# Finishing a block of nodes in stages, and scaling a relation's product after the matmul: a four-layer graph network on one core

## The chip, the core and the metric

The kernel runs on one core of a Trainium2 chip. Its engines are TensorE (PE in the profile, with its weight loads as PEld), VectorE (DVE), ScalarE (ACT), GpSimd (POOL) and SyncE (SP); each works through its own instructions in order. The metric is the device time of one execution in microseconds. Before the change its median over three runs is 2428.57 us (2426.19 to 2432.78).

## What is computed

Four graph layers over 3125 nodes of 128 features and 53,125 edges sorted by destination, each with a residual and a layer norm. Layer 0 is a GIN block of four rounds; layers 1 to 3 sum, for each destination node, what its edges bring by relation. Cut to the core:

```
x = layernorm(x + gin(x))                                  # 4 x: h = x + segment_sum(x[src], dst); relu(h W1 + b1) W2 + b2
# layer 1: mean per relation
out = x @ root + bias
for r in range(8):
    s = segment_sum((x @ W[r])[src] * (type == r), dst)
    c = segment_sum(type == r, dst)
    out = out + s / maximum(c, 1)
x = layernorm(x + relu(out))
# layer 2: relation weights from 8 bases, an attention factor per relation; x @ update once per edge of dst
x = layernorm(x + relu(layer2(x)))
# layer 3: messages (x[src] @ W[r] + bias_term[r]) * gate, plus x @ loop_weight
x = layernorm(x + relu(layer3(x)))
```

In layers 1 to 3 the kernel first sums the source rows per destination and relation (or basis) and multiplies by the relation's matrix afterwards, once per node instead of once per edge.

## The kernel before

A first part (`gnn_kernel`) tests that the edges are in order; they are, so `in_order` runs, and the other path (`any_order`) does not. `gin_layers` does layer 0: it builds the adjacency in SBUF as BF16 (lines 668 to 698) and multiplies densely (`dense`, line 598). It ends by writing the table `fx0` (`xtab[0]`) to HBM.

**One relational layer** (`relational`, line 945) walks over 416 tiles of 128 edges. For each tile GpSimd gathers the 128 source rows from the layer's table (line 915); four tiles share one buffer `xg`, and there are six such buffers, so gathers can run 24 tiles ahead. VectorE makes a one-hot `oh` of 128 edges by 16 destinations x 8 relations (lines 1003, 1005, 1010 for layers 1, 2, 3), TensorE multiplies (`pw`, line 1012, three PSUM buffers), and VectorE adds the 128x128 product into `sums` at a column offset read from a register (line 1014). `sums` holds features x (node, relation) for all nodes. Layers 1 and 3 also count edges (or sum gates) per node and relation on TensorE, `pc` at line 1020, from one-hots made by `hots` (line 918) for eight tiles at a time; the records show two per product, as for every FP32 matmul here.

**One block** is 128 nodes; there are 25 (24 full ones and one of 53). A block is complete after the last tile that can hold one of its destinations (`last_tile`, line 766). At that tile the loop at line 1022 calls the layer's `finish`, which emits everything for the block at once:

- `finish1` (line 1046): load the block's own rows `xb` (SP), copy the counts (ScalarE), reciprocals of max(count, 1) for 8 relations x 128 nodes; spread these over all partitions with eight selector matmuls (`sel`, line 1057) in two PSUM halves, and scale `sums` into `sc` (line 1058); turn the rows (`turned`, line 936); then one accumulation in PSUM: root, bias, and eight products (`by_relation`, line 1031); `normed` (line 1039) with residual and layer norm; store to `fx1`.
- `finish2` (line 1113): the same pattern without counts of its own; it multiplies by the update matrix and eight bases, norms, turns the result again, makes the gates of layer 3 (line 1126 on) and stores 136 columns to `gtab`.
- `finish3` (line 1135): loop weight, bias by summed gates, eight products, norm, store to the output.

After a block the loop clears the part of `sums` of the block before it (line 1026, `clear` on ScalarE). Layer 2's gathers read the table that layer 1's blocks write, all rows of it, so a layer's first gather waits for the last block's store.

The code is written in one order, and the framework then sets each engine's order of instructions, when the program is built, from dependencies and its own estimates of time. So instructions of a block's finish can stand between those of tiles, and the counts of layer 1 stand well ahead of the tiles that they belong to.

Of the kernel before, what the change touches and what calls it, by code (L numbers as in the profile page):

```python
# [58 lines left out]
NSEG = NB  # L59
NR = 8  # L60
DGRP = 16
DRIFT = 40.0
PADDST = 4095

# [701 lines left out]
def last_tile(c1):  # L766

    return max(t for t in range(TE) if low(t)[0] < c1)
# [8 lines left out]
def in_order(ctx: ExitStack, tc: tile.TileContext, a: dict, out: bass.AP, pre: dict):  # L777
# [31 lines left out]
    def clear(b, engine=nc.scalar.copy):  # L809
        engine(sums[:, b * P * NR:(b + 1) * P * NR], zero.to_broadcast([P, P * NR]))  # L810
# [29 lines left out]
    def load(name, shape, src):  # L840
        t = const.tile(shape, src.dtype, name="f_" + name)
        nc.sync.dma_start(t, src)
        return t
# [3 lines left out]

    rW = load("rW", [P, R8, D], a["L1_gnn_W"].rearrange("r i o -> i r o"))
    root = load("root", [P, D], a["L1_gnn_root"])
    rbias = load("rbias", [1, D], a["L1_gnn_bias"].rearrange("(a o) -> a o", a=1))  # L850
    sel = const.tile([R8, R8, P], F32, name="f_sel")
    cnt = const.tile([R8, NP], F32, name="f_cnt")
    zeroh = const.tile([1, SEGN + 2 * W], BF16, name="f_zeroh")
    nc.vector.memset(zeroh, 0.0)
# [60 lines left out]
        nc.gpsimd.indirect_dma_start(out=dst, out_offset=None, in_=table,  # L915
                                     in_offset=bass.IndirectOffsetOnAxis(ap=idx, axis=0))

    def hots(keys_, n, name, t):

        m = min(GRP, TE - t)  # L920
        oh = wk.tile([P, GRP, n], F32, name=name)
        nc.vector.tensor_tensor(oh[:, :m], iota[:, :n].unsqueeze(1).to_broadcast([P, m, n]),
                                keys_[:, t:t + m].unsqueeze(2).to_broadcast([P, m, n]), OP.is_equal)
        return oh
# [20 lines left out]
    def relational(layer, table, width, finish, beside=lambda t: None):  # L945
        counted = layer in (1, 3)
        segs, cgroups = {}, {}
        b = 0

        def coefficients(t):  # L950

# [13 lines left out]
        for t in range(TE):  # L965
# [4 lines left out]
            if t % GRP == 0:  # L970
                m = min(GRP, TE - t)
                if counted:
                    r8 = hots(et8, R8, "h8", t)
                    hw = hots(dlr, W, "hw", t)
                    spot = []
                    for i in range(2):
                        us = [u for u in range(t, t + m) if len(segments(u)) > i]
                        us = range(us[0], us[-1] + 1) if us else us
                        spot.append(dict(zip(us, values(seg[0:1, i, us[0]:us[-1] + 1], PE, [spots(u, i) for u in us]))) if us else {})
                else:  # L980
                    if t == 0:
                        coefficients(0)
                    if t + GRP < TE:
                        coefficients(t + GRP)
# [15 lines left out]
            for u, x, r, gate in ready:  # L1000
                oh = ohp.tile([P, W * NR], F32, name="oh")
                if layer == 1:
                    nc.vector.tensor_scalar(oh, iota[:, :W * NR], key8[:, u:u + 1], None, op0=OP.is_equal)  # L1003
                elif layer == 2:
                    nc.vector.scalar_tensor_tensor(  # L1005
                        oh.rearrange("p (d b) -> p d b", b=NR), W2["dcol"], dlr[:, u:u + 1],
                        cgroups[u - u % GRP][:, u % GRP, :].unsqueeze(1).to_broadcast([P, W, NBASE]),
                        op0=OP.is_equal, op1=OP.mult)
                else:
                    nc.vector.tensor_scalar(oh, iota[:, :W * NR], key8[:, u:u + 1], gate, op0=OP.is_equal, op1=OP.mult)  # L1010
                ps = psum.tile([P, W * NR], F32, name="pw", bufs=3)
                nc.tensor.matmul(ps, x[:, u % 4, :D], oh, start=True, stop=True)  # L1012
                w = sums[:, bass.ds(place[u % DGRP], W * NR)]
                nc.vector.tensor_tensor(w, ps, w, OP.add)  # L1014
                if counted:
                    for i, j in enumerate(segments(u)):
                        if j not in segs:
                            segs[j] = psum.tile([R8, SEGN + 2 * W], F32, name="pc", bufs=2)
                            nc.tensor.matmul(segs[j], zeroh[:, :R8], zeroh, start=True, stop=False)
                        nc.tensor.matmul(segs[j][:, bass.ds(spot[i][u], W)], r, hw[:, u % GRP, :], start=False,  # L1020
                                         stop=u == last_tile(min(N, (j + 1) * P)))
                while b < NB and u == last_tile(min(N, (b + 1) * P)):
                    finish(b, sums[:, b * P * NR:(b + 1) * P * NR].rearrange("p (d r) -> p r d", r=NR),
                           segs[b][:, W:W + P] if counted else None)
                    if layer < 3 and b > 0:
                        clear(b - 1)
                    b += 1
        if layer < 3:
            clear(NB - 1)

    def by_relation(s, w, first):

        pb = psum.tile([P, D], F32, name="pm", bufs=2)
        first(pb)
        for r in range(NR):
            nc.tensor.matmul(pb, s[:, r, :], w[:, r, :], start=False, stop=r == NR - 1)  # L1036
        return pb

    def normed(pb, xb, dst):

        r = wk.tile([P, 1, D], F32, name="res")
        nc.vector.scalar_tensor_tensor(r[:, 0, :], pb, 0.0, xb, op0=OP.max, op1=OP.add)
        layer_norm(nc, wk, eps, r, dst, P, 1)


    def finish1(b, s, pc):
        blk = slice(b * P, (b + 1) * P)
        xb = rows_of(xtab[0], b)
        nc.scalar.copy(cnt[:, blk], pc)
        ci = wk.tile([R8, P], F32, name="ci")  # L1050
        nc.vector.tensor_scalar(ci, cnt[:, blk], 1.0, None, op0=OP.max)
        nc.vector.reciprocal(ci, ci)
        sc = wk.tile([P, R8, P], F32, name="sc", bufs=1)
        for h in range(0, R8, BPB):
            pr = psum.tile([P, BANK], F32, name="pr", bufs=1)
            for r in range(BPB):
                nc.tensor.matmul(pr[:, r * P:(r + 1) * P], sel[:, h + r, :], ci, start=True, stop=True)  # L1057
            nc.vector.tensor_tensor(sc[:, h:h + BPB, :], s[:, h:h + BPB, :], pr.rearrange("p (r d) -> p r d", d=P), OP.mult)  # L1058
        xt = turned(xb)

        def first(pb):
            nc.tensor.matmul(pb, xt, root, start=True, stop=False)
            nc.tensor.matmul(pb, ones[0:1, :], rbias, start=False, stop=False)

        y = wk.tile([P, 1, D], F32, name="y")
        normed(by_relation(sc, rW, first), xb, y)
        nc.sync.dma_start(xtab[1][blk, :], y[:, 0, :])

    def beside1(t):
        if t == 0:  # L1070
            clear(1)
        if t == 4:
            nc.vector.tensor_copy(sel, ident[:R8, :R8].unsqueeze(2).to_broadcast([R8, R8, P]))
        if t == 120:
            later_weights()
        for b in range(2, NB):
            if t == max(1, first_tile(b * P) - GRP):
                clear(b)
# [34 lines left out]
    def finish2(b, s, _):  # L1113
        blk = slice(b * P, (b + 1) * P)
        xb = rows_of(xtab[1], b)
        xt = turned(xb)
        pd = psum.tile([P, P], F32, name="pm", bufs=2)
        nc.tensor.matmul(pd, ones[:R8, :], cnt[:, blk], start=True, stop=True)
        xd = wk.tile([P, P], F32, name="xd")
        nc.vector.tensor_tensor(xd, xt, pd, OP.mult)  # L1120
        pb = by_relation(s, W2["bases"], lambda pb: nc.tensor.matmul(pb, xd, W2["upd"], start=True, stop=False))
        yg = wk.tile([P, 1, GX], F32, name="yg")
        normed(pb, xb, yg[:, :, :D])
        xt = turned(yg[:, 0, :D])
        pg = psum.tile([P, P], F32, name="pm", bufs=2)
        nc.tensor.matmul(pg[:, :R8], xt, W2["V"], start=True, stop=True)
        gs = wk.tile([P, R8], F32, name="gs")
        nc.vector.tensor_tensor(gs, pg[:, :R8], W2["gconst"], OP.add)
        nc.scalar.activation(yg[:, 0, D:], gs, AF.Sigmoid)
        nc.sync.dma_start(gtab[blk, :], yg[:, 0, :])  # L1130

    relational(2, xtab[1][:, :], D, finish2)

# [1 line left out]
    def finish3(b, s, pc):  # L1135
        blk = slice(b * P, (b + 1) * P)
        xb = rows_of(gtab, b)
        cg = wk.tile([R8, P], F32, name="ci")
        nc.scalar.copy(cg, pc)
        xt = turned(xb)  # L1140

        def first(pb):
            nc.tensor.matmul(pb, xt, W2["gloop"], start=True, stop=False)
            nc.tensor.matmul(pb, cg, W2["gb8"], start=False, stop=False)

        y = wk.tile([P, 1, D], F32, name="y")
        normed(by_relation(s, W2["gW"], first), xb, y)
        m = min(P, N - b * P)
        nc.sync.dma_start(out[b * P:b * P + m, :], y[:m, 0, :])

    relational(3, gtab[:, :], GX, finish3)

# [134 lines left out]
```

## Time and profile before

| what | us |
|---|---|
| median of three runs | 2428.57 |
| profiled execution, its own time | 2915.92 |
| span of the profile (first to last instruction) | 2914.0 |
| mean granted TensorE clock in the profile | 0.669 |
| gathers of layer 1, 2, 3: first start to last start | 782.2 to 1476.3; 1514.9 to 2130.4; 2173.4 to 2876.0 |
| all gathers, busy | 795.7 (832 of layers 1 and 2) + 395.2 (416 of layer 3) |
| tile products, line 1012, busy / mean of one record | 669.8 / 0.410 |
| additions into `sums`, line 1014, busy / mean | 358.4 / 0.287 |
| selector matmuls, line 1057, busy / mean | 96.2 / 0.388 |
| scaling, line 1058, busy / mean | 53.9 / 1.078 |
| products by relation, line 1036, layers 1, 2, 3, busy | 91.4, 101.2, 100.1 |

The profile is of one execution under the profiler, which is 487 us longer than the median. A group line gives busy time and mean ns of one after the first bar, and after the second the idle time of the engine just before these instructions, with what ended it. "issue" means that the engine waited for nothing the profile shows. Matmul ends are modelled, not measured.

### The profile page before, as it was taken

How to read it: one execution, taken by the hardware profiler on the slowest of the kernel's cores; microseconds unless marked ns; L12 is line 12 of the kernel's file. 1: busy time of each engine (PE TensorE's matmuls, PEld its weight loads, DVE VectorE, ACT ScalarE, POOL GpSimd, SP SyncE). 2: the span in 40 equal slices, each digit the busy share in tenths (PEclk: the TensorE clock that was granted, in tenths of full speed). 3: DMA queues.
4: the chain of work that ended last, by engine and by line, in shares of the span. 5: the costliest groups of instructions: out<-in, count | busy, mean ns of one | idle time of the engine just before them, and what ended most of it. 6: DMA issues, size and time to landing. Idle time of an engine off the chain costs nothing.

```text
span 2914.0 us, 37334 instructions
## 1 busy us (share of the span) xinstructions
PE 1997.4 (69%) x10854; PEld 1388.4 (48%) x10898; DVE 1167.2 (40%) x4727; ACT 501.4 (17%) x1009; POOL 1194.6 (41%) x1259
## 2 busy tenths in 40 slices
PE   2899999999657667777664655565553655565556
PEld 1224344444345556566553545455543545454445
DVE  5782631112324444344442433443332433343334
ACT  2882731110210000000010222122120000000000
POOL 0000000000255555555636666666636555555553
PEclk7558689999755656566665666666665566566567
DMA  2000020111211111111111111111112121111111
GB/s 62 8 1 12 12 66 23 53 38 46 63 40 50 42 44 45 44 45 45 49 31 47 50 51 49 50 48 51 50 30 47 45 48 43 46 46 46 46 46 28
DMA packets 103154, 122.82 MB, mean 42 GB/s; under 512 B 25851, under 2 KB 82472, under 8 KB 102952
## 3 DMA queue, kind: packets, MB, share of 16 engines
q0 software_dynamic: 40000, 83.59, 11.5%
q1 hardware_dynamic: 51006, 28.49, 3.3%
q10 hardware_dynamic: 11946, 8.27, 0.9%
q8 instruction: 100, 1.64, 0.2%
q14 instruction: 102, 0.84, 0.1%
HBM read 104.98 MB, written 15.27 MB: 41 GB/s over the span
## 4 chain that ended last, share of the span: by engine, by line
PE 47%; another core or an unknown queue 19%; issue 15%; DVE 6%; POOL 6%; ACT 4%; DMA 3%; DVEq 0%; ACTq 0%; POOLq 0%; SPq 0%
PE acc L605 13%; PE pw L1012 12%; PE pm L1036 7%; POOL xg L915 6%; PE pa L682 4%; PE pc L1020 2%; ACT AT L691 2%; PE pr L1057 2%; DVE sums L1014 2%; PE pr L615 1%; PE pr L610 1%; DMA xg<-fx,f_srcI 1%; ACT sums L810 1%; DVE oh L1010 1%
## 5 line engine op out<-in xcount | busy, mean ns | idle before, releaser
L915 POOL DMA_INDIRECT xg<-fx,f_srcI x832 | 795.7, 956 | 1258.6 <-DMA f_ggb<-in_L_gnn_gate_bias_dram 742.5
L1012 PE MATMUL pw<-oh,xg 128*128 128x128 f32 x2496 | 669.8, 410 | 353.1 <-issue 143.9
L1012 PEld LDWEIGHTS pw<-oh,xg 128*128 128x128 f32 x2496 | 529.3, 286 | 439.2 <-issue 191.2
L1014 DVE TENSOR_TENSOR sums<-pw,sums 128x128 f32 x1248 | 358.4, 287 | 878.4 <-remote 390.4
L915 POOL DMA_INDIRECT xg<-gtab,f_srcI x416 | 395.2, 950 | 350.4 <-PE pw L1012 159.4
L605 PE MATMUL acc<-AT,xs 128*128 128x512 bf16 (+1 forms) x2056 | 404.7, 352 | 4.7 <-ACT AT L691 1.1
L605 PEld LDWEIGHTS <-xs 128*128 128x128 bf16 x2100 | 185.0, 98 | 221.5 <-issue 18.8
L682 PE MATMUL pa<-ohk,ohs 128*128 128x425 bf16 x416 | 205.7, 509 | 44.6 <-ACT AT L691 24.4
L691 ACT CAST AT<-pa 128x400 f32 x430 | 218.9, 520 | 47.2 <-PE pa L686 15.7
L680 DVE TENSOR_SCALAR ohk<-iotah,places 128x425 bf16<-128x425 f16 x416 | 139.5, 335 | 44.0 <-PE pa L686 29.6
L810 ACT COPY sums<-f_zero 128x1024 f32<-128x1024 f32 x74 | 75.2, 1042 | 371.6 <-PE pm L1036 135.7
L1005 DVE SCALAR_TENSOR_TENSOR oh<-f_dcol,edges,coef 128x128 f32<-128x128 f32 x416 | 136.9, 343 | 0.9 <-ACT coef L962 0.6
L1010 DVE TENSOR_SCALAR oh<-p_iota,edges,g 128x128 f32<-128x128 f32 x416 | 135.9, 353 | 0.0
L682 PEld LDWEIGHTS <-ohs 128*128 128x128 bf16 x416 | 43.7, 105 | 176.1 <-DVE ohk L680 128.8
L1020 PE MATMUL pc<-hw,h 128*8 128x16 f32 x1456 | 86.4, 186 | 58.3 <-issue 53.7
L1003 DVE TENSOR_SCALAR oh<-p_iota,edges 128x128 f32<-128x128 f32 x416 | 120.0, 295 | 0.0
L1057 PE MATMUL pr<-ci,f_sel 8*128 8x128 f32 x400 | 96.2, 388 | 33.4 <-DVE sc L1058 30.1
L1036 PE MATMUL pm<-f_gW,sums 128*128 128x128 f32 x400 | 100.1, 430 | 27.3 <-DVE sums L1014 27.3
L608 DVE COPY hT<-acc 128x512 f32<-128x512 f32 (+1 forms) x28 | 17.4, 622 | 251.4 <-PE acc L605 240.9
L1020 PE MATMUL pc<-hw,rg 128*8 128x16 f32 x1456 | 84.5, 182 | 43.9 <-issue 28.2
L1036 PEld LDWEIGHTS pm<-f_gW,sums 128*128 128x128 f32 x400 | 97.8, 336 | 28.7 <-DVE sums L1014 28.4
L1036 PE MATMUL pm<-f_bases,sums 128*128 128x128 f32 x400 | 101.2, 436 | 13.1 <-DVE sums L1014 7.6
(194 smaller groups left out, 1828.2 us busy)
## 6 DMA issues: line engine op xcount, KB each, us to landing
xg<-fx,f_srcI POOLq DMA_INDIRECT x832
xsd<-sp SPq DMA_DIRECT2D x18, 384.0 KB
xg<-gtab,f_srcI POOLq DMA_INDIRECT x416
xs<-xsd SPq DMA_DIRECT2D x9, 384.0 KB
xs<-xsd ACTq DMA_DIRECT2D x9, 384.0 KB
xb<-fx SPq DMA_DIRECT2D x49, 64.0 KB
gtab<-yg SPq DMA_DIRECT2D x25, 68.0 KB
fx<-y SPq DMA_DIRECT2D x25, 64.0 KB
```

The source lines that it names most:

```text
L605: nc.tensor.matmul(acc[:, :n], xs[s // BPB][:, s % BPB, i, :], AT[k][:, s, at:at + n], start=s == 0 and i == 0, stop=s == NB - 1 and i == 2)
L680: nc.vector.tensor_scalar(ohk, iotah, keyb[:, t:t + 1], None, op0=OP.is_equal)
L682: nc.tensor.matmul(ps, ohs, ohk, start=True, stop=t == 0)
L691: nc.scalar.copy(AT[k][:, :, bass.ds(og[k][t % GRP], W)], ps3[:, :, :W])
L915: nc.gpsimd.indirect_dma_start(out=dst, out_offset=None, in_=table, in_offset=bass.IndirectOffsetOnAxis(ap=idx, axis=0))
L1005: nc.vector.scalar_tensor_tensor(oh.rearrange("p (d b) -> p d b", b=NR), W2["dcol"], dlr[:, u:u + 1], cgroups[u - u % GRP][:, u % GRP, :]. ...
L1010: nc.vector.tensor_scalar(oh, iota[:, :W * NR], key8[:, u:u + 1], gate, op0=OP.is_equal, op1=OP.mult)
L1012: nc.tensor.matmul(ps, x[:, u % 4, :D], oh, start=True, stop=True)
L1014: nc.vector.tensor_tensor(w, ps, w, OP.add)
L1020: nc.tensor.matmul(segs[j][:, bass.ds(spot[i][u], W)], r, hw[:, u % GRP, :], start=False, stop=u == last_tile(min(N, (j + 1) * P)))
L1036: nc.tensor.matmul(pb, s[:, r, :], w[:, r, :], start=False, stop=r == NR - 1)
L1057: nc.tensor.matmul(pr[:, r * P:(r + 1) * P], sel[:, h + r, :], ci, start=True, stop=True)
```

## The change

Each `finish` becomes a generator. `relational` starts it `AHEAD` = 5 tiles before the block's last tile and advances every open block by one stage per tile (`step`). A stage that yields "sums" is not passed before the block's last tile. After the last tile the rest is run stage by stage over all open blocks. Every layer's `clear` now stands inside its block's stages.

```
+        def step(u):
+            for entry in list(blocks):
+                last, stages = entry
+                if u < last and entry in waits:
+                    continue
+                try:
+                    if next(stages) == "sums":
+                        waits.append(entry)
+                except StopIteration:
+                    blocks.remove(entry)
...
-                while b < NB and u == last_tile(min(N, (b + 1) * P)):
-                    finish(b, sums[:, b * P * NR:(b + 1) * P * NR].rearrange("p (d r) -> p r d", r=NR),
-                           segs[b][:, W:W + P] if counted else None)
-                    if layer < 3 and b > 0:
-                        clear(b - 1)
+                while b < NB and u >= last_tile(min(N, (b + 1) * P)) - AHEAD:
+                    blocks.append((last_tile(min(N, (b + 1) * P)), finish(b, sums_of(b), lambda j=b: segs[j][:, W:W + P])))
                     b += 1
-        if layer < 3:
-            clear(NB - 1)
+                step(u)
+        while blocks:
+            step(TE)
```

In layer 1 the products are made from the unscaled `sums`, four relations to a PSUM bank, and VectorE scales them while it adds them up; counts are transposed to nodes x relations first. The bias is loaded to all partitions and starts the sum. The one-hots of the counts are BF16 in this layer.

```
+        xb = rows_of(xtab[0], b)
+        yield
+        yield
+        xt = turned(xb)
+        yield "sums"
+        nc.scalar.copy(cnt[:, blk], pc())
+        yield
+        pt = psum.tile([P, P], F32, name="pm", bufs=2)
+        nc.tensor.transpose(pt[:, :R8], cnt[:, blk], ident[:R8, :R8])
+        ci = wk.tile([P, R8], F32, name="ci")
+        nc.vector.tensor_scalar(ci, pt[:, :R8], 1.0, None, op0=OP.max)
+        nc.vector.reciprocal(ci, ci)
+        acc = rbias
         for h in range(0, R8, BPB):
+            yield
+            pr = psum.tile([P, BPB, D], F32, name="pr", bufs=1)
             for r in range(BPB):
-                nc.tensor.matmul(pr[:, r * P:(r + 1) * P], sel[:, h + r, :], ci, start=True, stop=True)
-            nc.vector.tensor_tensor(sc[:, h:h + BPB, :], s[:, h:h + BPB, :], pr.rearrange("p (r d) -> p r d", d=P), OP.mult)
+                nc.tensor.matmul(pr[:, r, :], s[:, h + r, :], rW[:, h + r, :], start=True, stop=True)
+            if h:
+                clear(b)
+                pb = psum.tile([P, D], F32, name="pm", bufs=2)
+                nc.tensor.matmul(pb, xt, root, start=True, stop=True)
+            yield
+            for r in range(BPB):
+                v = wk.tile([P, D], F32, name="acc")
+                nc.vector.scalar_tensor_tensor(v, pr[:, r, :], ci[:, h + r:h + r + 1], acc, op0=OP.mult, op1=OP.add)
+                acc = v
+        v = wk.tile([P, D], F32, name="acc")
+        nc.vector.tensor_tensor(v, pb, acc, OP.add)
+        yield
+        y = wk.tile([P, D], F32, name="y")
+        yield from normed(v, xb, y)
+        nc.sync.dma_start(xtab[1][blk, :], y)
```

`normed` yields once, between the square root on ScalarE and the reciprocal. `finish2` and `finish3` keep their operations and are cut by `yield` in the same way: rows, turned rows, (layer 2: update) "sums", four products, four products, norm, and in layer 2 turning, gate product, gates and store, each a stage. In layer 3 the bias product comes after the eight products instead of before them.

## The prediction

> **What bounds it now.** I read the page's busy shares first, then the gathers of each layer by their line, then who they waited for, and last the two drains between layers in order of time.
>
> ```profile
> span 2914.0 us, 37334 instructions
> PE 1997.4 (69%) x10854; PEld 1388.4 (48%) x10898; DVE 1167.2 (40%) x4727; ACT 501.4 (17%) x1009; POOL 1194.6 (41%) x1259
> ...
> PEclk7558689999755656566665666666665566566567
> ```
>
> No engine is above 69%, and by that row TensorE leads. But busy shares hide a pace. The three relational layers each issue 416 gathers on GpSimd, and the rows of the gather line, asked for in the windows of layers 1, 2 and 3, give their first and last start:
>
> ```profile
> L915 POOL DMA_INDIRECT xg<-fx,f_srcI x416: 942/947/1679, 782.2 to 1476.3; - x139
> L915 POOL DMA_INDIRECT xg<-fx,f_srcI x416: 942/947/1400, 1514.9 to 2130.4; - x139
> L915 POOL DMA_INDIRECT xg<-gtab,f_srcI x416: 942/947/1194, 2173.4 to 2876.0; - x139
> ```
>
> What GpSimd waited for, in total us, times and longest:
>
> ```profile
> POOL xg L915 <- PE pw L1012: 332.2, 96, 9.1
> POOL xg L915 <- issue: 322.7, 1050, 0.9
> ```
>
> A gather takes 0.947 us, and 322.7 us over 1050 waits is 0.31 us to the next: 1.252 us per gather when nothing holds it. 415 steps of 1.252 are 519.6 us per layer, but the layers took 694.1, 615.5 and 702.6 us from first to last gather. So GpSimd was held for 174.5 + 95.9 + 183.0 = 453 us, mostly until TensorE gave a gather buffer back (24 tiles fit in the buffers). The rest of the 2914 us: 782 us before the first gather, and three drains without any gather: 1476.3 to 1514.9 (38.6 us), 2130.4 to 2173.4 (43.0), 2876.0 to the end (38.0).
>
> **The profile against the median.** The profiled execution took 2915.92 us by its own clock, 487 us over the median of 2428.57. The holds look like the difference. In many stretches TensorE's records creep:
>
> ```profile
> 799.23 0.18 PE L1020 MATMUL pc<-hw,h 128*8 128x16 f32 x1 [1.92 <-issue]
> 799.96 0.19 PE L1020 MATMUL pc<-hw,h 128*8 128x16 f32 x1 [0.54 <-issue]
> 802.07 0.18 PE L1020 MATMUL pc<-hw,h 128*8 128x16 f32 x1 [1.92 <-issue]
> ```
>
> These count matmuls wait for nothing ("issue") yet come 0.7 to 2.1 us apart, where others of this line come 0.02 to 0.07 us apart. I take these for a cost of recording. Without holds the profile would be 2914 - 453 = 2461 us, 32 us above the median; with drains of 29 instead of 40 us it is the median. So my reading of the timed runs: **GpSimd's gathers set the pace in all three layers**, 782 + 3 x 520 = 2342 us, and 2428.6 - 2342 = 87 us are drains and what holds are left. That is an estimate; no trace of a timed run exists.
>
> Here a rule of the Trainium skill points elsewhere. Perfetto Trace Analysis, section "Identifying the Most-Contended Engine", measures GpSimd by occupancy and TensorE by the busy share of its weight loads. In layer 1 (1000 to 1400 us by windows) these are 53 to 61% and 58 to 61%: level, and no engine near its limit. By that rule the time lies in gaps, and closing them could bring up to the 453 us of holds. By the gather row GpSimd stands at its pace at 0.947 / 1.252 = 76%, since the 0.31 us between gathers count as idle, and only the drains are left to gain from. I take the row, because it alone adds up to the median.
>
> **The change, part by part.** A block is 16.6 tiles, which is 20.8 us of gathers; that is the budget of every other engine per block.
>
> Layer 1, TensorE at its slow clock, by starts 0.21 us apart per record of 128x128. Before: tiles 33.3 x 0.21 = 7.1; counts 58 x 0.07 = 4.1; 16 selector records 3.4; 16 records of products 3.4; root, bias, transpose 1.1: 19.1 us. The change drops the selector (3.4) and bias (0.4), halves the count records by BF16 (2.0), and adds a transpose of 8x128 (0.2): 13.5 us. The products read sums in steps of 8 elements as stationary operand; layers 2 and 3 do so already, at 430 to 436 ns a record against 402, so at most +0.5.
> VectorE, layer 1, per block:
>
> ```profile
> L1058 DVE TENSOR_TENSOR sc<-sums,pr 128x512 f32<-128x512 f32 x50 | 53.9, 1078 | 32.7 <-PE pr L1057 26.0 <-PE pm L1036 4.1 <-PE pc L1020 2.6
> L1052 DVE RECIPROCAL ci<-ci 8x128 f32<-8x128 f32 x25 | 23.3, 933 | 0.0
> L1042 DVE SCALAR_TENSOR_TENSOR res<-pm,xb 128x128 f32<-128x128 f32 x75 | 21.7, 289 | 199.1 <-PE pm L1036 91.4 <-remote 54.1 <-PE pc L1020 21.0
> ```
>
> Gone are 2 x 1.08 + 0.93 + 0.22 = 3.3 us; new are 8 scale-and-adds at 0.289 (the row of line 1042 has the same form, PSUM and SBUF in), one add at 0.287, and a maximum and a reciprocal of 128x8 at 0.17 and 0.16 (rows of lines 1128 and 755): 2.9 us. Both engines were below 20.8 us and stay so: **nothing gained in mid-layer** while the pace is the gathers'; without that cover TensorE's 5.6 us x 25 = 140 us would show.
>
> Layers 2 and 3 keep their instructions; they are moved. The block's rows are loaded 5 tiles (6 us) ahead: 0.33 us on SP each, the same alternation with the result's store, so nothing waits longer. Transposes follow 2 tiles later, so TensorE no longer stands for the copy: in layer 3 that wait (line 1143) is 69.5 us in 18 times, and that for the counts 50.4 in 8. Under the gathers' pace these are worth nothing either, until TensorE's layer 3 block (7.1 + 4.1 + 3.4 + 1.1 = 15.7) with 5 us of waits comes to 20.7 against 20.8: just at the edge, so I leave 0 to 20 us for holds that really existed and take 6. Clearing moves from a block later to just behind the products: ScalarE's 1.04 us copy then waits for TensorE up to 3.9 us, and behind it stand turned rows and, in layer 2, coefficients, which are made 8 to 16 tiles (10 to 20 us) ahead. Covered. New waits: VectorE's scale-and-adds wait for four products (1.7 us) twice per block, and behind them the tile's additions; VectorE has about 12 us of work and 3.4 of waits in 20.8. Covered, bounded by 0 and 85 us in layer 1; I take 0.
>
> The clock speaks against spreading. Granted clock in the layers is 0.55 to 0.68, full for some 7 us after each block's burst of products, and 1.00 through 400 to 770 us. TensorE: Matmul & The Clock Gate, section "What's actually happening", says that after about 3.4 us of sustained work the clock doubles and an idle window halves it. Thin products spread over ten tiles would then never be sustained, and the clock goes to 0.50. By the rule TensorE loses up to half of a 7 us window per block, 3.4 us; my 13.5 and 15.7 us are already at the slow clock, so it costs nothing in the sum.
>
> **The drains** are where it counts. Layer 1 into 2, then 2 into 3, in order of time:
>
> ```profile
> 1488.95 4.05 PE L1012 MATMUL pw<-oh,xg 128*128 128x128 f32 x20 [0.82 <-DVE sums L1014]
> 1510.11 0.32 SPq L1067 DMA_DIRECT2D fx<-y  x1
> 1512.56 0.86 POOL L915 DMA_INDIRECT f_xs<-fx,f_esrc  x1 [35.35 <-issue]
> ...
> 2153.02 0.39 PE L1012 MATMUL pw<-oh,xg 128*128 128x128 f32 x2
> 2163.95 0.29 DVE L1042 SCALAR_TENSOR_TENSOR res<-pm,xb 128x128 f32<-128x128 f32 x1 [4.66 <-PE pm L1036]
> 2170.93 0.32 SPq L1130 DMA_DIRECT2D gtab<-yg  x1
> 2173.36 0.95 POOL L915 DMA_INDIRECT xg<-gtab,f_srcI  x1 [42.03 <-DMA gtab<-yg]
> ```
>
> Layer 1: the last tile's product ends at 1493.0, the last store is issued at 1510.1: 17.1 us, in which blocks 23 and 24 go through selector, scaling, products one after the other. In the changed program's order of instructions 16 products stand behind the last tile: four groups of 4, each 1.8 to 2.0 us, plus about 0.3 for the last scale-and-add before the one bank is free: 9; then add, residual, norm, store: 0.3 + 0.3 + 0.3 + 0.2 + 0.3 + 0.2 + 0.3 and hops: 2.5. 11.5 to 12: **-5 us**.
> Layer 2: from 2153.4 to 2170.9 are 17.5 us: block 23's norm, gate and two table loads of 1.28, and only then block 24's products. In the new order block 24's products follow block 23's at once, both norms go side by side, with one table load: 3.9 + 1.6 + 0.4 + 0.3 + 0.6 + 0.2 + 1.3 + 0.2 and 0.8 of hops: 9.3. **-8 us**.
> Layer 3 ends on 16 products and a norm in both orders; the bias product moves behind: +0.4. **0**.
> Sum: -5 - 8 - 6 = -19 us: 2428.6 - 19 = 2410.
>
> **Rivals.** (a) *No effect to see*, 2427: stages are spaced in an order fixed beforehand, and if the engines' real times differ, the drains' 13 us are lost in new waits. For it: the tail is short work with many hops. Against: the steps that go (selector, 10 us of a second norm and gate) stand in the chain one after the other. 0.20.
> (b) *The holds are real*, 2360: if the part before the first gather is shorter in timed runs by some 50 us, then 55 us of holds plus 13 of drains go. For it: the 120 us of waits in layer 3. Against: the creeping records. 0.15.
> (c) *Slower*, 2460: the new order keeps VectorE waiting for TensorE at the slow clock at every stage (four products, counts, root, norm), additions queue behind, three PSUM buffers fill, and TensorE stops too. It decides once these waits pass 20.8 - 12 = 9 us per block, which is 6 stages at 1.5 us; at 11 us it costs 2 x 25 = 50 us in layer 1, less the drains: some 2460. Against: two waits of 1.7 are all I can name. 0.15.
>
> **Numbers.** My case has 0.50: 2410, by itself 2398 to 2423. A change below 0.3%, 7.3 us, can't be told from none. Faster: (b) 0.15 and nearly all of mine, 0.64 together; same: (a), 0.21; slower: (c), 0.15. The range 2355 to 2432 leaves out (c) and the far end of (b).
>
> **What would show it.** Steps of 1.25 us between gathers as before; the gaps at the layers' ends about 5 and 8 us shorter; granted clock nearer 0.5; TensorE's waits of lines 1143 and 1144 gone; the profiled time may fall by more than the timed one, since holds fall with TensorE's records. I am wrong if the timed run falls by over 50 us (then the holds were real), or if VectorE's waits on the new product bank grow to several us per block.

## The result, and the profile after

The changed kernel takes 2425.59 us (median of 20 runs, 2422.17 to 2429.00), the kernel before, beside it, 2430.51 us (20 runs, 2426.19 to 2435.95): a ratio of 0.9982, 95% interval 0.9975 to 0.9989. It is 4.9 us faster; 2410 was forecast. Two later sets of runs gave 0.9982 (0.9973 to 0.9990) and 0.9983 (0.9977 to 0.9990).

In some sets of runs every run of the kernel before takes about 2914 us in place of 2430; the profile of before that the prediction read was taken in that condition, the timed runs and the profile after were not, and so the trace of before to compare with is a later one, from a set in which it takes 2430 us (experiment 1).

The page of the changed kernel:

```profile
span 2423.3 us, 35231 instructions
PE 1954.7 (81%) x9701; PEld 1329.0 (55%) x9745; DVE 1162.7 (48%) x4901; ACT 497.2 (21%) x1007; POOL 1193.0 (49%) x1259
...
PEclk9998968999998556666555556666566556556667
```

The span is 2423.3 us (2425.13 by the execution's own clock). TensorE is busy 81% of it and GpSimd 49%. The gather line's rows in layers 1, 2 and 3 (least, median and greatest ns, first and last start):

```profile
L915 POOL DMA_INDIRECT xg<-fx,f_srcI x416: 940/944/1550, 786.8 to 1308.4; - x139
L915 POOL DMA_INDIRECT xg<-fx,f_srcI x416: 940/944/1204, 1336.0 to 1860.7; - x139
L915 POOL DMA_INDIRECT xg<-gtab,f_srcI x416: 940/944/1051, 1880.0 to 2399.7; - x139
```

And what GpSimd waited for (total us, times, longest):

```profile
POOL xg L915 <- issue: 309.9, 1017, 0.3
POOL xg L915 <- PE pw L1028: 33.8, 111, 0.3
```

The longest single wait for TensorE inside a layer is 0.3 us, where the profile ahead of the prediction had 9.1: the gathers run at 1.25 us a step from the first to the last in all three layers. A gather is busy for 0.944 us of each step, so GpSimd is at its full pace while it counts as 76% busy.

### The profile page after: what moved, and what is told of

Read it like the earlier page. It is cut to its first block, busy times and chain, and to the rows that moved or that the text cites. A ratio compares the mean times of both kernels' runs of the same rounds, so it can differ in the third digit from the quotient of the medians.

```text
span 2423.3 us, 35231 instructions
## 1 busy us (share of the span) xinstructions
PE 1954.7 (81%) x9701; PEld 1329.0 (55%) x9745; DVE 1162.7 (48%) x4901; ACT 497.2 (21%) x1007; POOL 1193.0 (49%) x1259
## 5 line engine op out<-in xcount | busy, mean ns | idle before, releaser
L1028 PE MATMUL pw<-oh,xg 128*128 128x128 f32 x2496 | 724.0, 424 | 232.6 <-DMA xg<-fx,f_srcI 110.1
L1028 PEld LDWEIGHTS pw<-oh,xg 128*128 128x128 f32 x2496 | 546.5, 290 | 366.3 <-DVE sums L1030 144.8
L609 DVE COPY hT<-acc 128x512 f32<-128x512 f32 (+1 forms) x28 | 17.4, 621 | 252.8 <-PE acc L606 242.3
L1036 PE MATMUL pc<-hw,rg 128*8 128x16 f32 x1456 | 90.6, 186 | 59.0 <-DVE rg L1008 29.7
L1087 PE MATMUL pr<-f_rW,sums 128*128 128x128 f32 x400 | 109.5, 444 | 11.2 <-DVE acc L1095 11.0
L1036 PEld LDWEIGHTS pc<-hw,rg 128*8 128x8 f32 x1456 | 64.0, 90 | 96.1 <-issue 48.1
L1019 DVE TENSOR_SCALAR oh<-p_iota,edges 128x128 f32<-128x128 f32 x416 | 111.9, 295 | 0.0
L687 PE MATMUL pa<-ohk,ohs 128*128 x415 | 99.0, 239 | 15.5 <-issue 14.3
L1087 PEld LDWEIGHTS pr<-f_rW,sums 128*128 128x128 f32 x400 | 99.6, 334 | 15.7 <-DVE acc L1095 14.5
```

What stands on the lines that cost most here:

```text
L1087: nc.tensor.matmul(pr[:, r, :], s[:, h + r, :], rW[:, h + r, :], start=True, stop=True)
```

## Experiment 1: the kernel before, again

Edit: none. Two runs, in different sets.

> The kernel before, unchanged, for a trace without the creeping TensorE records. Theory A (the gathers set the pace in all three layers before and after, the change acts on the drains alone): each layer's gathers run at 1.25 us a step, 519 to 525 us from first to last, and what is left to the span (2428 - 785 - 3 x 521 = 80 us) is in the three gaps without gathers, against 27.6 + 19.3 + 23.6 = 70.5 us in the changed kernel. Rival B (holds are real before, and the change removes them while something else gives the time back): at least one layer takes over 530 us from first to last gather, with waits for TensorE over 10 us in sum.

> The kernel before, unchanged, for its trace. On a chip where it takes 2428 us, Theory A: layers of 519 to 525 us from first to last gather, and three gaps without gathers of together 75 us, 5 us more than the changed kernel's 70.5. On a chip where it takes 2914: layers of 694, 616 and 702 us as before.

The first took 2911.39 us, with layers of 694.0, 616.1 and 702.2 us, beside 11 runs of the kernel before of 2908.68 to 2925.48. There Theory A misses and Rival B's holds are real. The second took 2431.39 us, beside 24 runs of 2426.10 to 2433.76. Its gather rows:

```profile
L915 POOL DMA_INDIRECT xg<-fx,f_srcI x416: 941/947/1696, 782.2 to 1306.8; - x139
L915 POOL DMA_INDIRECT xg<-fx,f_srcI x416: 941/947/1409, 1332.1 to 1858.7; - x139
L915 POOL DMA_INDIRECT xg<-gtab,f_srcI x416: 941/947/1063, 1884.7 to 2405.3; - x139
```

Beside the rows after, with the two spans (2429.6 and 2423.3 us), that gives every term of the difference between these two traces, which is 6.3 us where the medians differ by 4.9:

| stretch, us | forecast | before | after | difference |
|---|---|---|---|---|
| start to first gather | 0 | 782.2 | 786.8 | +4.6 |
| layer 1, first to last gather | | 524.6 | 521.6 | -3.0 |
| gap between layers 1 and 2 | -5 | 25.3 | 27.6 | +2.3 |
| layer 2, first to last gather | | 526.6 | 524.6 | -2.0 |
| gap between layers 2 and 3 | -8 | 26.0 | 19.3 | -6.7 |
| layer 3, first to last gather | | 520.6 | 519.7 | -0.9 |
| last gather to the end | 0 | 24.2 | 23.6 | -0.6 |
| three layers together | -6 | 1571.8 | 1565.9 | -5.9 |
| all | -19 | 2429.6 | 2423.3 | -6.3 |

At 2430 us, where the result was taken too, Theory A's layers (519 to 525) are met within 2 us and its gaps (75 us; 25.3 + 26.0 + 24.2 = 75.5) to the microsecond, and Rival B has no hold to stand on. The three layers' difference is in part a matter of the step: its median was 1.252 us in this trace and 1.249 in that one, 415 x 0.003 = 1.2 us a layer, which leaves some 2 us. A trace of the new order with a step of 1.252 (experiment 3, second run) has 1567.7 us in the three layers, 4.1 less than before. So 2 to 4 us are left for the layers. Whether the step itself belongs to the change is not shown: the three traces of before have 1.252 and the three of the changed kernel 1.249, but the ring of experiment 3 has had both.

## Experiment 2: the changed kernel, again

Edit: none. Two runs.

> The changed kernel, unchanged. The runs so far showed that the kernel before takes 2428 us on one chip and 2914 on another, with the same program: on the second the TensorE products come back late by 2 to 9 us now and then and hold the gathers by some 450 us. Theory D (on a chip with holds the change saves time in mid-layer too, since it gives TensorE less to do; on one without, only the drains count): 2850 to 2865 us where before takes 2914, ratio 0.978 to 0.983; 2425 where before takes 2429. Rival B (the pauses are a cost that no order of instructions can move): at most 10 us off before on either chip.

> The changed kernel, unchanged, beside the run after it. If before takes about 2430 us here: 2425 a third time. If before takes 2914 (where the changed kernel has not run yet), Theory D (TensorE's late products hold the gathers there, and what the change takes from TensorE comes back as time): layer 1's arithmetic alone was -32 to -38 us, stages in layers 2 and 3 alone -21; the change has both, so -50 to -60, 2855 to 2865. Rival B: at most -10.

The changed kernel took 2426.02 us (13 runs) and 2425.79 us (21 runs), beside 2430.51 and 2429.89 before. First gathers at 785.8 and 787.8 us, gaps of 27.3 and 19.1, and of 27.5 and 19.1 us: the table's two gaps and its later start are no chance. The changed kernel itself never ran beside 2914 us, so Theory D stays open for it. One thing in the first of these expectations is not so: it lays the two times of before to two chips, but the chip with number 11 on record gave 2914 us in the set of the first run of experiment 1 and 2430 us in that of the second.

## Experiment 3: layer 1's products in the tiles' ring

The gap between layers 1 and 2 in the changed kernel, in order of time (start, length, engine, line; in brackets the idle time before it, and who ended it):

```profile
1312.14 0.77 PE L1028 MATMUL pw<-oh,xg 128*128 128x128 f32 x2 [0.74 <-DMA xg<-fx,f_srcI]
1312.70 2.09 PE L1087 MATMUL pr<-f_rW,sums 128*128 128x128 f32 x8
1314.83 0.35 DVE L1095 SCALAR_TENSOR_TENSOR acc<-pr,ci,f_rbias 128x128 f32<-128x128 f32 x1 [3.10 <-PE pr L1087]
...
1316.46 2.29 PE L1087 MATMUL pr<-f_rW,sums 128*128 128x128 f32 x8 [1.67 <-DVE acc L1095]
...
1320.35 2.27 PE L1087 MATMUL pr<-f_rW,sums 128*128 128x128 f32 x8 [1.60 <-DVE acc L1095]
...
1324.49 2.30 PE L1087 MATMUL pr<-f_rW,sums 128*128 128x128 f32 x8 [1.86 <-DVE acc L1095]
...
1326.83 1.51 DVE L1095 SCALAR_TENSOR_TENSOR acc<-pr,ci,acc 128x128 f32<-128x128 f32 x4 [1.79 <-PE pr L1087]
...
1330.55 0.32 SPq L1102 DMA_DIRECT2D fx<-y  x1
1333.71 0.85 POOL L915 DMA_INDIRECT f_xs<-fx,f_esrc  x1 [24.33 <-issue]
```

The four groups of products start at 1312.7, 1316.5, 1320.4 and 1324.5: 3.9 us apart, though a group takes 2.1 to 2.3. The first scale-and-add (line 1095) starts when all eight records are in, the four take 1.5 us, and only then is the one bank free: TensorE stands for 1.6 to 1.9 us each time ("DVE acc"). From the first group to the last scale-and-add that is 15.6 us. Before the change the same stretch was filled otherwise (the later trace of before):

```profile
1310.40 0.77 PE L1012 MATMUL pw<-oh,xg 128*128 128x128 f32 x2 [1.39 <-DMA xg<-fx,f_srcI]
1311.10 2.07 PE L1057 MATMUL pr<-ci,f_sel 8*128 8x128 f32 x8
1313.10 3.78 PE L1036 MATMUL pm<-f_rW,sc 128*128 128x128 f32 x16
...
1316.81 2.07 PE L1057 MATMUL pr<-ci,f_sel 8*128 8x128 f32 x8
...
1320.04 2.07 PE L1057 MATMUL pr<-ci,f_sel 8*128 8x128 f32 x8 [1.16 <-DVE sc L1058]
...
1322.04 3.39 PE L1036 MATMUL pm<-f_rW,sc 128*128 128x128 f32 x16
...
1327.32 0.32 SPq L1067 DMA_DIRECT2D fx<-y  x1
```

From the last tile's product to the last store it is 16.2 us there and 17.6 in the changed kernel. Edit, which gives the products the three banks of the tiles (the "ring") in place of one bank of their own:

```diff
-                ps = psum.tile([P, W * NR], F32, name="pw", bufs=3)
+                ps = psum.tile([P, BPB, D], F32, name="pw", bufs=3)[:, 0, :]
...
-            pr = psum.tile([P, BPB, D], F32, name="pr", bufs=1)
+            pr = psum.tile([P, BPB, D], F32, name="pw", bufs=3)
```

> The changed kernel with layer 1's products written into the ring of three banks that the tiles use, in place of one bank of their own, so that a group of products need not wait for the scale-and-adds of the group before. Theory A (the drain between layers 1 and 2 is long because products and scale-and-adds take turns, 4 x 4.0 us where TensorE alone needs 4 x 1.9): the drain is 5 to 7 us shorter, the kernel 2418 to 2421 us, -10 to -12 us against before. Rival C (the loss lies in mid-layer): no more than 2 us off 2425, or slower, since tiles now share their banks with the products.

> The changed kernel with layer 1's products written into the tiles' ring of three banks, a second time, now beside the changed kernel on the same chip. Theory A (products and scale-and-adds take turns on one bank in the drain between layers 1 and 2, 4 x 4.0 us): that drain is 5 to 7 us shorter than in the changed kernel, and so is the time, on either chip. Rival C (the drain is bound by the chain behind the products): 0 to 2 us.

The first took 2850.59 us beside 2913.89, ratio 0.9773 (0.9753 to 0.9793); its forecast, made for 2430 us, can't be read from it. The second: 2419.20 us beside 2430.51, ratio 0.9955 (0.9941 to 0.9969), 6.8 us less than the changed kernel in the same set. Its gap:

```profile
1311.44 7.73 PE L1087 MATMUL pw<-f_rW,sums 128*128 128x128 f32 x32
...
1324.02 0.34 DVE L1065 TENSOR_SCALAR y<-res,mv,rs 128x128 f32<-128x128 f32 x1
1326.75 0.86 POOL L915 DMA_INDIRECT f_xs<-fx,f_esrc  x1 [18.56 <-issue]
```

All 32 records of products now go as one stretch of 7.7 us, and the gap is 21.8 us, 5.5 less than the changed kernel's 27.3 in that set. Of these 5.5 us, 4.9 lie between the last tile's product and the last store (17.6 and 12.7 us) and 0.5 between that store and the next gather (2.9 and 2.4 us). So the turns on the one bank cost some 5 us, as Theory A said (5 to 7). The gap between layers 2 and 3 was also 1.5 us shorter (17.6 against 19.1), and not by the bank: the stretch behind the last tile's product is 9.2 us in both, but block 23's products start 1.3 us after the last gather's start in the ring's trace and 2.7 in the changed kernel's, so the two programs' order of instructions differs there.

## Experiment 4: four stages per tile at the layers' ends

Edit, on top of the ring:

```diff
-            for entry in list(blocks):
+            for entry in list(blocks) * (1 if u < last_tile(N - TAIL) else 4):
                 last, stages = entry
+                if entry not in blocks:
+                    continue
```

> As the run before it, and from the last tiles of each layer on every block takes four stages per tile instead of one, so that block 23's products stand before the last tile's product and not behind it. Theory A (both blocks' 32 records of products, 32 x 0.24 = 7.7 us, stand behind the last tile in the drains between layers 1, 2 and 3): up to 2 to 4 us less per drain between layers, 4 to 8 us less in all than the run with the ring. Rival (the sums that block 23 needs come with the last tiles, so its products can't start sooner): 0 to 2 us.

2424.62 us (ratio 0.9977, 0.9968 to 0.9985): 5.4 us slower than the ring alone, which neither theory expected. The gap between layers 1 and 2 is 1.2 us shorter (20.6), that between layers 2 and 3 is 6.2 us longer (23.8), nearly the 26.0 of before the change. First the kernel before there (the trace of experiment 1), then the changed kernel, then this run:

```profile
1864.34 0.39 PE L1012 MATMUL pw<-oh,xg 128*128 128x128 f32 x2
...
1864.54 0.29 DVE L1042 SCALAR_TENSOR_TENSOR res<-pm,xb 128x128 f32<-128x128 f32 x1 [3.41 <-PE pm L1036]
...
1871.39 3.91 PE L1036 MATMUL pm<-f_bases,sums 128*128 128x128 f32 x16
...
1875.34 0.29 DVE L1042 SCALAR_TENSOR_TENSOR res<-pm,xb 128x128 f32<-128x128 f32 x1 [4.59 <-PE pm L1036]
...
1882.32 0.32 SPq L1130 DMA_DIRECT2D gtab<-yg  x1
```

```profile
1867.66 0.64 PE L1028 MATMUL pw<-oh,xg 128*128 128x128 f32 x2
...
1867.90 0.29 DVE L1056 SCALAR_TENSOR_TENSOR res<-pm,xb 128x128 f32<-128x128 f32 x1 [1.59 <-PE pm L1051]
...
1868.68 3.89 PEld L1051 LDWEIGHTS pm<-f_bases,sums 128*128 128x128 f32 x16 [0.68 <-DVE sums L1030]
...
1872.80 0.29 DVE L1056 SCALAR_TENSOR_TENSOR res<-pm,xb 128x128 f32<-128x128 f32 x1 [3.76 <-PE pm L1051]
...
1875.95 1.90 SPq L1176 DMA_DIRECT2D gtab<-yg  x2
```

```profile
1859.68 0.29 DVE L1058 SCALAR_TENSOR_TENSOR res<-pm,xb 128x128 f32<-128x128 f32 x1 [3.66 <-PE pm L1053]
...
1865.34 0.32 SPq L1178 DMA_DIRECT2D gtab<-yg  x1
1868.91 0.29 DVE L1058 SCALAR_TENSOR_TENSOR res<-pm,xb 128x128 f32<-128x128 f32 x1 [4.26 <-PE pm L1053]
...
1875.74 0.32 SPq L1178 DMA_DIRECT2D gtab<-yg  x1
```

Before, block 24's products start 6.9 us after block 23's residual, when that block's norm and gate have gone through TensorE, and the residuals are 10.8 us apart. In the changed kernel the products follow at 0.8 us and the residuals are 4.9 us apart; both stores are in one row at 1875.95 (issued within 1.9 us). With four stages per tile the residuals are 9.2 us apart again. So what the change gains here is that two blocks go side by side, and the spacing of one stage per tile is what does it.

## Experiment 5: each part alone

Edits: the kernel before with the change's layer 1 (BF16 counts, bias on all partitions, the lines of the new `finish1` without their yields); and the changed kernel with layer 1 as before, in one go at the block's last tile. The core of the first, then of the second:

```diff
-                nc.tensor.matmul(pr[:, r * P:(r + 1) * P], sel[:, h + r, :], ci, start=True, stop=True)
-            nc.vector.tensor_tensor(sc[:, h:h + BPB, :], s[:, h:h + BPB, :], pr.rearrange("p (r d) -> p r d", d=P), OP.mult)
+                nc.tensor.matmul(pr[:, r, :], s[:, h + r, :], rW[:, h + r, :], start=True, stop=True)
+            for r in range(BPB):
+                v = wk.tile([P, D], F32, name="acc")
+                nc.vector.scalar_tensor_tensor(v, pr[:, r, :], ci[:, h + r:h + r + 1], acc, op0=OP.mult, op1=OP.add)
+                acc = v
```

```diff
     def finish1(b, s, pc):
         blk = slice(b * P, (b + 1) * P)
+        yield "sums"
         xb = rows_of(xtab[0], b)
...
```

> The kernel before with layer 1's new arithmetic alone (BF16 counts, products first, scaled by VectorE), no stages. Theory A (only the drain between layers 1 and 2 can feel it; there each group of 4 products and its 4 scale-and-adds take turns on one bank, 4.0 us a group, 16 us for two blocks, where selector, scaling and products took about as long before): -3 to +4 us against before. Rival C (the stages gained the 19 us of the forecast and the new work on VectorE gave 14 of them back in mid-layer): +10 to +15 us, with holds in layer 1's gathers.

> Layer 1's new arithmetic alone, a second time, to see it where the kernel before takes about 2430 us. Theory A: no holds to save there; the first gather comes 3 to 4 us later, since with this arithmetic the framework puts four row loads ahead of the last store of layer 0's table on SyncE; the drain between layers 1 and 2 is 1 to 4 us longer (products and scale-and-adds take turns, and the blocks one after the other): +4 to +8 us against before. Rival C (new work on VectorE holds the gathers): over +10 us, with layer 1's gathers over 530 us. If the chip is in the condition of the first call, again 0.987.

> Layer 1's new arithmetic alone. If before takes about 2430 us here, Theory A: first gather 3 to 4 us later, drain between layers 1 and 2 longer by 1 to 4 us, no holds: +4 to +8 us. Rival C: over +10 us. If before takes 2914: 0.988 for the third time.

> The changed kernel with layer 1's arithmetic as before, each block of it finished in one go at its last tile; stages in layers 2 and 3 alone. Theory A: the whole gain of the change lies in the drain between layers 2 and 3: -3 to -7 us against before, about 2425. Rival C: the stages alone bring what the forecast had for layers 2 and 3, -14 us or more, 2416 or less.

> Stages in layers 2 and 3 alone, layer 1 as before, a second time. Theory A (the change's whole gain is the drain between layers 2 and 3, where the two last blocks' norms, gates and table loads now go side by side): that drain 19 us against 26.0, all else as before: -6 to -8 us, so more than the whole change. Rival (the gain needs layer 1's part too): -3 us or less. In the condition of the first call again 0.993.

> Stages in layers 2 and 3 alone. If before takes about 2430 us here, Theory A: drain between layers 2 and 3 of 19 us against 26.0, all else as before: -6 to -8 us. Rival: -3 us or less. If before takes 2914: 0.993 for the third time.

All six ran beside 2914 us. The first run of each misses what Theory A expected; the later four came as their expectations had it for 2914 us. Layer 1 alone: ratios 0.9868 (0.9845 to 0.9891), 0.9890 (0.9871 to 0.9909) and 0.9885 (0.9865 to 0.9905), 32 to 38 us off 2914. Layer 1's gathers took 645 to 650 us against 694. Stages alone: 0.9927 (0.9907 to 0.9946), 0.9936 (0.9922 to 0.9951) and 0.9921 (0.9900 to 0.9942), 21 us. There the gathers wait for TensorE (343.5 us in 103 waits in the first run of experiment 1), and what is taken from TensorE comes back as time; there the holds of the prediction's rival (b) are real.

The times say nothing on Theory A at 2430 us, but the stretch from a layer's last tile product to its last store can be read in these traces too. Between layers 2 and 3 it is 17.4 to 17.5 us with layer 1 alone and 8.9 to 9.4 us with stages alone, against 17.5 to 17.6 in all traces of before and 9.1 to 9.2 in the changed kernel: the gain of that gap comes with the stages and needs nothing of layer 1. Between layers 1 and 2 it is 17.7 to 17.8 us with layer 1 alone and 17.6 in the changed kernel: the long stretch comes with the new arithmetic, and the stages do not shorten it. (With layer 1 as before it was 13.4 to 17.1 us, depending on the trace.)

## Experiment 6: SyncE's order before the first gather

The first gather waits for the last store of layer 0's table: in the traces that store has landed at 781.2 us before and 785.7 after the change, and the first gather starts 1.0 and 1.1 us later. SyncE's instructions around it, with VectorE's last instruction on the rows that are stored, in the kernel before (the later trace) and in the changed one:

```profile
775.27 0.33 DVE L757 TENSOR_SCALAR y<-xn,ln_mv,ln_rs 53x128 f32<-53x128 f32 x1
775.43 0.58 SPq L842 DMA_DIRECT2D f_gW<-in_L_gnn_W_dram  x1
...
777.34 0.25 SPq L737 DMA_DIRECT2D fx<-y  x1
777.70 1.94 SPq L933 DMA_DIRECT2D xb<-fx  x4
```

```profile
772.11 1.38 SPq L933 DMA_DIRECT2D xb<-fx  x3
...
777.39 0.33 DVE L758 TENSOR_SCALAR y<-xn,ln_mv,ln_rs 53x128 f32<-53x128 f32 x1
...
779.53 0.58 SPq L843 DMA_DIRECT2D f_gW<-in_L_gnn_W_dram  x1
780.21 0.39 SPq L738 DMA_DIRECT2D fx<-y  x1
```

Before, the four row loads of layer 1 (xb) stand behind the store; after the change they stand ahead of it, three from 772.1 on, the fourth at 774.7. The rows that the store writes are ready at 775.6 before and 777.7 after, so the store goes 1.7 us after its rows before and 2.5 us after the change; and the load of 128x8x128 weights (gW) is issued 0.7 us ahead of it and not 1.9. From rows ready to first gather: 6.6 us before, 9.1 after. In all six traces with the old layer 1 it is 6.6 to 7.0, whether before takes 2430 or 2914 us, and in all nine with the new one and SyncE's order as built 9.1 to 9.9; layer 1's arithmetic alone has it too, so it comes with that part and not with the earlier start of the blocks. Edit, on top of the ring (first run the rows only, second run both):

```diff
+        pre["stored"] = nc.cur_bb.bb.instructions[-1]
...
-        xb = rows_of(xtab[0], b)
+        with tc.issue_after(pre["stored"]):
+            xb = rows_of(xtab[0], b)
...
-            later_weights()
+            with tc.issue_after(pre["stored"]):
+                later_weights()
```

> The kernel with the ring, and layer 1's row loads kept behind the last store of layer 0's table on SyncE, which gives SyncE the order that it had before the change. Theory A: the first gather returns from 786 to 782 us after the start: 3 to 4 us less than with the ring alone, 2415 to 2416. Rival E (the later start is from the larger bias load or chance): no change, 2419.

> As the run before it, and the loads of later weights stand behind that last store too, so that SyncE issues it as soon as its rows are ready and no other transfer shares its landing. Theory A (the store is issued late because of the queue, and lands late because of the transfers issued just before): first gather at 778 to 781 us, 1 to 4 us less again. Rival: the store's rows are ready no sooner than its turn on SyncE: 0.

> Ring, and layer 1's row loads behind the last store of layer 0's table. If before takes about 2430 us here, Theory A: first gather at 782 us, 2415 to 2416. Rival E: 2419, as with the ring alone. If before takes 2914: 0.974 again.

> As the run before it, with the later weights behind that store too. If before takes about 2430 us here, Theory A: first gather at 778 to 781 us, 2412 to 2415. Rival: no less than the run before it. If before takes 2914: 0.972 again.

All four ran beside 2914 us, so their times don't speak for 2430: rows behind 2839.01 and 2833.96 us (0.9738, 0.9715 to 0.9761; 0.9724, 0.9704 to 0.9743), all behind 2833.20 and 2833.14 (0.9723, 0.9706 to 0.9741; 0.9722, 0.9699 to 0.9745). In the times the two edits can't be told apart. The stretch itself can be read in any trace: from rows ready to first gather 7.0 and 6.5 us with the rows behind, 3.7 and 3.7 with all behind. For the stretch, Rival E (the larger bias load, which stays) and the last rival fall: the order on the queue sets it.

## Experiment 7: the three mends together

Edit: the ring; rows and weights behind the store; four stages per tile in layer 1 alone.

> The changed kernel with all three mends: products in the tiles' ring; rows and later weights behind the last store of layer 0's table on SyncE; and in layer 1 alone four stages per tile from block 23's last tile on. If before takes about 2430 us here, Theory A: 5.5 us less for the drain between layers 1 and 2 with the ring, about 1 more with four stages, 5 to 6 for the first gather (3.7 us behind the rows' readiness against 9.2): 2412 to 2415, 11 to 14 us less than the changed kernel. Rival: the earlier start meets the layer's first loads and is lost again, 2418 to 2420. If before takes 2914: 2830 to 2840.

2412.40 us (5 runs, 2411.47 to 2412.58), ratio 0.9928 (0.9915 to 0.9942): 13.4 us less than the changed kernel in the same set and 17.5 less than before, as Theory A had it. The store in its trace, and the first gather:

```profile
777.16 0.24 SPq L738 DMA_DIRECT2D fx<-y  x1
780.85 1.10 POOL L916 DMA_INDIRECT xg<-fx,f_srcI  x1 [740.90 <-DMA f_comp<-in_L_gnn_comp_dram]
```

From rows ready to first gather it is 3.7 us. (The row names another load as what ended the wait; the store itself has landed at 779.6 us.) The gaps are 20.9 and 17.7 us, the rest as in the changed kernel.

## Why the forecast was off

- **What bounds it** was right: the gathers' step of 1.25 us in every layer, and the gaps are what can be gained. At 2430 us, 782.2 + 1571.8 + 75.5 us of gaps add up to the span, as the estimate of 2342 + 87 had it. In layer 1 TensorE is busy for 411 us after the change and 456 before (from the first gather to the last), and the layer got 3.0 us shorter. The rule that was weighed against it (the Trainium skill, Perfetto Trace Analysis, "Identifying the Most-Contended Engine") was used on the profile at 2914 us and gave up to 453 us of holds to gain. At 2430 us the three layers take 1571.8 us where 1245 steps of 1.252 are 1558.7, so only 13 us of holds were there.
- **The records that creep as a cost of recording** was wrong. They come with the condition at 2914 us: unchanged, the kernel took 2914 us (medians) in three more sets of runs, timed ones. The number that it led to (no holds in the timed runs) was right, by luck.
- **"16 products stand behind the last tile: four groups of 4, each 1.8 to 2.0 us, plus about 0.3 for the last scale-and-add before the one bank is free: 9"** is the step that failed. A group is 2.1 to 2.3 us, and none of its scale-and-adds starts before all of it is in; then four of them follow, 1.5 us together (0.34 each, costed at 0.289), not the last one's 0.3: 15.6 us in place of 9. From the last tile's product (ended 1312.9) to the store 17.6 us went by where 11.5 to 12 were forecast. Before it was 16.2 and not the 17.1 of the profile that was read. So this stretch got 1.5 us longer, the store took 0.7 more to the next gather (3.2 against 2.4, cause open), and the gap came out 2.3 longer and not 5 shorter. The ring, which takes the turns away, brings the stretch to 12.7.
- **"The same alternation with the result's store, so nothing waits longer"** failed too, elsewhere: the first four row loads passed the last store of layer 0 on SyncE's queue. That is 2.5 us by the stretch from rows ready; the rest of the table's 4.6 is when the rows were ready in that run.
- **Holds, -6**: -2 to -4, once the two runs' steps are set apart. The waits of lines 1143 and 1144 (69.5 and 50.4 us in the profile that was read) come to 12.0 and 2.4 us, weight loads included, in the later trace of before, and to 6.9 and 0 from these causes in the changed kernel: there was little to gain.
- **The drain of layer 2, -8**: -6.7. The mechanism and the sum were right: from the end of the last tile's product (1868.3) to the last store (1877.5) it is 9.2 us, forecast 9.3, against 17.6 before (1864.7 to 1882.3). Left out was that this last product itself comes later: it ends 7.6 us after the last gather's start, and 6.0 before. Block 23's products stand ahead of it in both, but after the change they start 2.6 us after that gather and not 1.9, and a tile's product stands between their two halves.
- **Layer 3's end, 0**: -0.6. **VectorE's new waits**: 55.7 us in 39 times for the products in layer 1, 2.2 us a block where 3.4 were costed; covered.
- **The clock** was to go nearer to 0.50 by the rule weighed there (the Trainium skill, TensorE: Matmul & The Clock Gate, "What's actually happening"). The granted clock in layers 1, 2 and 3 was 0.66, 0.61 and 0.66 before and 0.60, 0.61 and 0.62 after: a little lower, and without cost. The rule is not at odds with the trace: after the change the clock still stands at 0.50 for a while (1005.1 to 1022.1 us) and then at 1.00 (1022.2 to 1028.9). That the spread products would never be sustained work was the wrong part.

With the terms as measured: -19 + 7.3 (first gap) + 2.5 (queue) + 4 (holds, at -2) + 1.3 (second gap) - 0.6 (layer 3's end) = -4.5; the measured difference is -4.9. That is the forecast's rival (a) in size and half in kind: the first gap lost its gain to a new wait, the second kept most of it.

## What to carry over

Where an engine off the critical path sets the pace, cost a change by the stretches in which that engine does nothing, and there write out every hand-over: a group on one bank costs the producer and all its consumers one after the other, not the longer of the two. When instructions move, look at the order that each queue gets as built, before the first of them too: four small loads that pass one store cost half as much as the change gained in all. And when a profile's own time is 20% off the timed median, take a second profile before reading waits from the first.

## What was not expected of the hardware

In the condition at 2914 us TensorE's records start 0.7, 1.4 or 2.1 us apart at places where they wait for nothing. The first run of experiment 1, and below it the later trace of before, where 18 of these count products take 1.2 us:

```profile
798.59 0.18 PE L1020 MATMUL pc<-hw,h 128*8 128x16 f32 x1 [1.22 <-issue]
800.01 0.18 PE L1020 MATMUL pc<-hw,h 128*8 128x16 f32 x1 [1.24 <-issue]
802.11 0.19 PE L1020 MATMUL pc<-hw,h 128*8 128x16 f32 x1 [1.91 <-issue]
```

```profile
797.73 1.21 PE L1020 MATMUL pc<-hw,h 128*8 128x16 f32 x18 [0.65 <-issue]
```

VectorE's additions also start late after the last tile product that ended before them (ends are modelled): where VectorE had been idle and the lag was above 0.2 us, the lags sum to 195, 245 and 188 us in the three layers of the profile ahead of the prediction, and to 9, 8 and 6 in the later trace. The mean granted clock is little lower (0.669 against 0.706). What sets the condition stays open; the chip alone does not (experiment 2).

Second: how long a store takes to land goes with what was issued just ahead of it. From the last store of layer 0 to the first gather it was 3.7 us with no weights just ahead of it, 4.7 to 5.1 with the 512 KB of gW 1.6 to 2.1 us ahead, 6.5 to 7.4 with gW 0.7 us ahead. That gW itself is the cause was not shown, since other loads moved with it.

Third: the gathers' median step was between 1.249 and 1.252 us, and changed from run to run of the same program (1.249 and 1.252 in the ring's two).
